# Order of work in a four-layer transformer kernel: a rate for each sequence, and six small shifts

## The chip, the cores and the metric

The kernel runs on one core of a Trainium2 chip. The metric is the device time of one execution in microseconds, from start to end, median of several runs. A core has five engines with a queue of instructions each, worked off in order: TensorE (PE; its weight loads are listed apart as PEld), VectorE (DVE), ScalarE (ACT), GpSimd (POOL), and SyncE (SP), which here only issues transfers. Layers are counted from 1 in the text and from 0 in the code (`l`), sequences likewise (`b`).

## The reference

Four transformer blocks, one after the other, on x of 4 sequences x 512 tokens x 288 channels in float32, with 16 heads of 18, an MLP of 1152, and shift, scale and gate rows computed from a condition vector:

```python
x = _L0_cond_ref(...)   # softmax attention over the tokens; MLP = 4 experts, the 2 best of each token
x = _L1_cond_ref(...)   # softmax attention over the tokens; MLP with gelu
x = _L2_cond_ref(...)   # attention over the heads, token by token (below); MLP with gelu
x = _L3_cond_ref(...)   # softmax attention over the tokens; MLP with gelu

# in _L2_cond_ref: each token's 16 heads attend to one another
attn = jnp.einsum('nthd,ntkd->nthk', q * scale, k)
attn = jax.nn.softmax(attn, axis=-1)
out = jnp.einsum('nthk,ntkd->nthd', attn, v)
out = out.transpose(0, 2, 1, 3).reshape(n, t, d)
x = x + gate_msa[:, None, :] * (out @ proj_w + proj_b)
```

Each block is x + gate * attention(modulate(layernorm(x))) and then x + gate * mlp(modulate(layernorm(x))). In the first block the gate logits choose two experts for each token, and their softmax (the "shares") weighs the two outputs.

## The kernel before, in words

**A planner writes the order.** The program of each engine is laid out in advance by a planner with a counter, `flow["now"]`, that goes up by one at each *gap*. The main line of work (attention steps, expert blocks, MLPs) emits matmuls and calls `gap` or `whole_products` between them; there, side work is put in. Side work stands in lists of generators (`products` for TensorE work; `lanes`, `moves`, `loads`, `spreads`, `casts` for the rest), each with a due time and the keys it reads. `mark(key, delay)` makes a key ready `delay` gaps later; a task starts when its keys are ready. `fill` takes pieces until their costs have used the budget `us` (1.0 for `lanes` and `moves`); a task that is late (due + `SLACK` of 8 gaps passed) goes on until the budget is down to `flow["least"]`. A piece that yields `WAIT` ends that call, so the next piece comes a gap later. Nothing of this costs time on the chip; only the order it leaves counts: what stands ahead of what in each engine's queue.

**Layer 1.** Attention over tokens runs in steps, two gaps each: scores, maxima on VectorE (`maxima`, L721), exponents on ScalarE (L749), value products (L777). A unit is four heads of a sequence and has four steps; its queries and keys come packed by product, and are spread to rows of 32 by transfers (`spread`, L701) issued on SP and POOL. Beside the first steps run the norm of sequence 2, the loads of the projection on POOL (L349 to L355), the clearing of the memory for tokens by expert (L1326, L1332), the product of the gate row (`gate_product`), and the rows for all modulations, half a layer at a time: `load_modulation` (three weight tiles of 288 KB, L405 to L407) and `modulation` (18 matmuls L423, three adds L429, rows written to memory by SP, L479). The next half's loads wait until the half before is `modulated`.

The experts' MLPs follow as 19 blocks of 256 tokens (`expert_block`), each three rounds of "up" (L1710, L1716), gelu on ScalarE (L1722, `hid_b`) and "down" (L1730); a block is 18 gaps. Beside the first blocks the last sequence's tokens are placed, listed (`listing`, VectorE) and scattered, and its shares are computed (`share`: subtract on VectorE L1517, exponent on ScalarE L1519, products on VectorE). `gather` and `combine` bring the outputs back to x, on POOL and VectorE, from block 11 on.

**Layers 2 and 3.** Layer 2's attention is like layer 1's. The MLP of its first sequence is put inside the attention. The MLPs of its sequences 2 to 4, and then all of layer 3's, run as halves of 256 tokens (`half_mlp`: up L1918, L1925, gelu L1929, down L1940; 36 gaps for a sequence; x is updated by ScalarE L1951 and POOL L1952, L1953). Beside them runs layer 3's attention over heads, called the images here: 16 tiles of 128 tokens, each with three products q, k, v (`kept`, L1005), four products and sums on VectorE (`weigh`, L1020, L1026), a softmax (L1030, L1032, exponent on ScalarE L1193), four products with v on POOL (`weighted`, L1039) and their sums on VectorE (`summed`, L1051). After every fourth tile `after(b)` reads the sequence back (L1069), turns and projects it, and norms it for the MLP. The norm of the next sequence (`before(b)`) starts when x of the layer before is marked. These norms compute statistics on VectorE (L512, L513), 1/sqrt on POOL (L520 to L523), and apply them on ScalarE (L537, `xh`), several gaps later (`lag`).

`follow`, called at each gap, keeps the images in step: a credit goes up by `flow["rate"]` at each gap and down by each piece's cost, about VectorE's time for it; pieces that give TensorE work have a negative cost. While it is positive, pieces are emitted.

```python
flow["credit"] = min(flow["credit"] + flow["rate"], 3.0)
...
flow["credit"] -= cost
```

**Layer 4** is again attention over tokens and MLPs. Its first norm and first queries and keys are put beside the end of layer 3's MLPs; its spreads use the tiles that held the images' q, k and v, so they come after the images' end.

The names that the change touches: `RATE`, `flow["rate"]`, `flow["least"]` (in `steps`, `expert_block`), the due time of `norm(l, 0, b)` in `attention`, `share`, the mark of x in `half_mlp`, and the due times of `gate_product` and of the first `modulation` behind the layers' loop.

Of the kernel before, what the change touches and what calls it, by code (L numbers as in the profile page):

```python
# [48 lines left out]
BT = 2 * P  # L49
N_BLOCKS = 2 * B * S // BT + NE - 1  # L50
INSIDE = (44,)
RATE = 1.35
SLACK = 8
EARLY = 5
SHORT = (EARLY + 1, EARLY + 3)
# [5 lines left out]
def tile_dit_blocks(ctx: ExitStack, tc: tile.TileContext, x_in, cond_t, sel_den, sel_b, w_gate, layers, out):  # L61
# [543 lines left out]
    def attention(l, start):  # L605
# [232 lines left out]
        def steps(inside=None, tail=None):  # L838

            end = N_STEPS - LEAD  # L840
            if hidden:
                ready_now = ("set", l, 0)
                while ready.get(ready_now, 1 << 30) > flow["now"]:
                    gap(0.5)
                rebase(start)
            close_all()

            def sum_pair(step, to):
                sum_values(step - 1, to, True, False)
                sum_values(step, to, False, True)  # L850

            flow["least"] = -0.8
            for step in range(first_step, N_STEPS + 1):
                odd = step % 2
                if step == end - 2:
                    flow["least"] = -1e9
                mark(("step", l, step), 0)
                if step < end:
                    flow["others"], flow["turn"] = ((4, 5, 6, 7) if odd and step > 0 else (0, 1, 2, 3)), -1
                if step < 0:  # L860
                    maxima(step, 4 if odd else 0, (4,))
                    flow["others"] = (0, 1, 2, 3) if odd else (4, 5, 6, 7)
                    whole_products(0.4)
                elif step < end:
                    if odd:
                        maxima(step, 4, (1, 1, 2))
                        weights(step, (0, 1, 2, 3), (2, 2))
                        whole_products(1.7)
                    else:
                        weights(step, (0, 1, 2, 3), (1, 1, 2))  # L870
                        maxima(step, 4, (4,))
                        if step:
                            sum_pair(step - 1, other())
                        whole_products(0.3)
                    if inside is not None and step in inside:
                        now = flow["now"]
                        flow["others"] = (7,)
                        inside[step]()
                        close_all()
                        rebase(now)  # L880
                else:
                    if step == end:
                        flow["others"] = (6, 7)
                        if tail is not None:
                            tail()
                    if step < N_STEPS:
                        weights(step, (3, 4, 0, 1), (2, 2))
                    if step == end:
                        sum_pair(step - 1, SUMS)
                    else:  # L890
                        c = (step - 1) % TB
                        sum_values(step - 1, SUMS, c == 0 or step - 1 == end, c == TB - 1)
                    gap(PACE[0])
                    gap(PACE[1])
            close_all()
# [20 lines left out]
        for b in range(B):  # L916
# [1 line left out]
            last = s0 + NG * TB  # L918
            first = hidden and b == 0
            task(  # L920
                lanes, start - 70 if first else at_step(s0 - LEAD - 9 if b else s0 - LEAD - 6),
                [("x", l, 0, b)] + ([("scattered", B - 1)] if l == 1 else []) + ([("step", l, 0)] if b else []),
                norm(l, 0, b, 10 if first and prev == OVER_HEADS else 3),
            )
# [586 lines left out]
    def share(b):  # L1511

        l = lg[:, b * TB : (b + 1) * TB, :]
        both = blocks.pop(("both", b))
        top = tiny([TB, 1], "top")
        nc.vector.tensor_reduce(top, l, AX.X, ALU.max)
        nc.vector.tensor_tensor(l, l, top.to_broadcast([P, TB, NE]), ALU.subtract)  # L1517
        yield 0.4
        nc.scalar.activation(l, l, AF.Exp)  # L1519
        nc.vector.tensor_tensor(l, l, both, ALU.mult)  # L1520
        yield 0.4
        nc.vector.tensor_reduce(top, l, AX.X, ALU.add)
        nc.vector.reciprocal(top, top)
        yield 0.4
        nc.vector.tensor_tensor(l, l, top.to_broadcast([P, TB, NE]), ALU.mult)
        sel = tiny([2, TB, NE], "sel2")
        nc.vector.tensor_tensor(
            sel, chosen[:, :, b * TB : (b + 1) * TB, :], l.unsqueeze(1).to_broadcast([P, 2, TB, NE]), ALU.mult
        )
        yield 0.4  # L1530
        nc.vector.tensor_reduce(shares[:, :, b * TB : (b + 1) * TB], sel, AX.X, ALU.add)
        mark(("shares", b))
        yield 0.4
# [158 lines left out]
    def expert_block(i):  # L1692


        PY, UP = 0, 2
        US = 0.5
        n = tiles_of(i)
        cols = slice(0, n * P)

        def wait_for(key):  # L1700
            while ready.get(key, 1 << 30) > flow["now"]:
                gap(US)

        def up(g, fs):
            wait_for(("third", 3 * i + g))
            rest, b1 = thirds[i][:2]
            w1 = thirds[i, g][0]
            for j in range(3):
                for k in range(KF):
                    nc.tensor.matmul(  # L1710
                        banks[:, UP + j, cols], w1[:, k, j * P : (j + 1) * P], hx[i][:, k, cols], start=k == 0, stop=False
                    )
                gap(US)
            for j in range(3):
                r = slice(j * RC, (j + 1) * RC)
                nc.tensor.matmul(banks[:, UP + j, cols], rest[r, g, :], hx[i][r, KF, cols], start=False, stop=True)  # L1716
            if g == 2:
                mark(("block read", i), 0)
            hid = []
            for j, f in enumerate(fs):  # L1720
                t = work.tile([P, S], F32, tag="ot", bufs=7, name=f"hid_b{i}_{f}")[:, cols]
                nc.scalar.activation(t, banks[:, UP + j, cols], AF.Gelu_apprx_tanh, bias=b1[:, f : f + 1])  # L1722
                hid.append(t)
            return hid

        def down(g, fs, hid):
            w2 = thirds[i, g][1]
            for j, f in enumerate(fs):
                for t in range(n):
                    nc.tensor.matmul(  # L1730
                        banks[:, PY + t, :C], hid[j][:, t * P : (t + 1) * P], w2[:, j, :], start=f == 0, stop=f == NF - 1
                    )
                if f < NF - 1:
                    gap(US)
            mark(("third free", 3 * i + g), 0)
            if g == 2:
                y = blocks["y", i] = work.tile([P, 2, C], F32, tag="upd", bufs=2, name=f"y_b{i}")
                nc.vector.tensor_tensor(
                    y[:, :n], banks[:, PY : PY + n, :C],
                    blocks.pop(("b2", i)).unsqueeze(1).to_broadcast([P, n, C]), ALU.add,  # L1740
                )
                mark(("block out", i))
                gap(US)

        wait_for(("turned", i))
        flow["most"] = -0.05
        for g, fs in enumerate(TRIOS):
            hid = up(g, fs)
            if pending_down:
                pending_down.pop()()  # L1750
            pending_down.append(lambda g=g, fs=fs, hid=hid: down(g, fs, hid))
        flow["most"] = -1e9
# [153 lines left out]
    def half_mlp(l, b, half, hook=None):  # L1906
# [26 lines left out]
        def down(fs, hid):  # L1933
# [14 lines left out]
            if fs[-1] == NF - 1:  # L1948
# [3 lines left out]
                nc.gpsimd.tensor_tensor(y, y, gate[:, b : b + 1, :].to_broadcast([P, 2, C]), ALU.mult)  # L1952
                nc.gpsimd.tensor_tensor(x[:, t0 : t0 + 2, :], x[:, t0 : t0 + 2, :], y, ALU.add)  # L1953
                if half == 1:
                    mark(("x", l + 1, 0, b), 5)
                gap(US)

        for fs in DUOS:
# [47 lines left out]
    for l in range(n_layers):  # L2006
# [7 lines left out]
        if l == 0:  # L2014
            task(products, -100, [("xh", 0, 0, 0)], modulation(l, 0, range(2)))
            task(loads, base, [("spread", l, 2)], load_projection(l))
            task(products, base + 14, [("mod", l, 0), ("ada", 0, 0, 2), ("step", 0, 1)], gate_product(l, 0))
            halves = [(m // 2, m % 2) for m in range(1, 2 * n_layers)]
            for i, half in enumerate(halves):
                free = [("step", 0, 7 * i + 1)] + ([("modulated",) + halves[i - 1]] if i else [])  # L2020
                at = base + 2 * (LEAD + 7 * i) + 2
                task(casts, at, free, load_modulation(*half, range(3), "w2"))
                task(products, at + 10, [("ada",) + half + (2,), ("gate row", 0, 0)], modulation(*half))
        before = [("x", l - 1, 1, B - 1)] if l else []
        task(casts, base + 20, [("gate row", l, 0)] + before + ([("step", 0, 6)] if l == 0 else []), gating(l, 0))
        before = [("x", l, 0, B - 1)] if l else []
# [66 lines left out]
        chain.append([attention_over_heads(OVER_HEADS), False])  # L2093

    lead_attention(1, inside={step: lambda b=b: early_mlp(b) for b, step in enumerate(INSIDE)}, tail=begin_chain)
    flow["rate"] = RATE
    flow["others"] = (4, 7)
    for b in range(len(INSIDE), B):
        while ready.get(("ht", 1, 1, b), 1 << 30) > flow["now"]:
            gap(0.5)  # L2100
        for half in range(2):
# [110 lines left out]
```

## Time and profile before

| | us |
|---|---|
| median of 3 runs | 2200.44 (2199.94 to 2205.9) |
| the profiled execution | 2201.77 |
| its span, first to last instruction | 2200.1 |
| TensorE busy in it | 2050.1 (93%) |
| VectorE busy | 1069.3 (49%) |
| ScalarE busy | 813.9 (37%) |
| POOL busy | 539.9 (25%) |
| granted TensorE clock, mean | 0.973 |

The stages in the span, by the lines that run in them: attention of layer 1 to about 425 us, expert blocks to 847, attention of layer 2 (with one MLP inside) to about 1230, MLPs of layers 2 and 3 with the images to about 1705, attention of layer 4 to about 2050, its MLPs to the end.

In the profile's lists a group reads: line, engine, operation, what it writes and reads; how often; busy time and mean; and the idle time of the engine just before, with what ended it. In a list of waits, "A x L1 <- B y L2: total, times, longest" says that engine A idled before its instruction of line L1 until engine B's of L2 was done. In a table of stretches each engine's busy microseconds and instructions stand in the order PE, weight loads, DVE, ACT, POOL, then the granted clock, the transfers' share and GB/s. In a timeline each row has start, duration, engine, line, and in brackets the idle time before it and what ended it.

### The profile page before, as it was taken

How to read it: one execution, taken by the hardware profiler on the slowest of the kernel's cores; microseconds unless marked ns; L12 is line 12 of the kernel's file. 1: busy time of each engine (PE TensorE's matmuls, PEld its weight loads, DVE VectorE, ACT ScalarE, POOL GpSimd, SP SyncE). 2: the span in 40 equal slices, each digit the busy share in tenths (PEclk: the TensorE clock that was granted, in tenths of full speed). 3: DMA queues.
4: the chain of work that ended last, by engine and by line, in shares of the span. 5: the costliest groups of instructions: out<-in, count | busy, mean ns of one | idle time of the engine just before them, and what ended most of it. 6: DMA issues, size and time to landing. Idle time of an engine off the chain costs nothing.

```text
span 2200.1 us, 28964 instructions
## 1 busy us (share of the span) xinstructions
PE 2050.1 (93%) x10782; PEld 1157.2 (53%) x10782; DVE 1069.3 (49%) x1656; ACT 813.9 (37%) x1333; POOL 539.9 (25%) x584
## 2 busy tenths in 40 slices
PE   7899999899999898999999999889899999999997
PEld 2334434367777474344454677656567444443554
DVE  4556667442002404576445769599630555664101
ACT  2434443422222123545435332333332555455111
POOL 2312131231004013020011295778611101001101
PEclk9989999999999999999999999989999999999999
DMA  3253212355666353000000000312210100000000
GB/s 82 70 171 119 63 57 37 105 167 167 199 200 200 100 167 102 26 24 18 18 6 20 18 9 17 60 26 33 30 48 8 48 20 17 14 18 1 9 14 22
DMA packets 171770, 139.13 MB, mean 63 GB/s; under 512 B 80605, under 2 KB 153749, under 8 KB 171630
## 3 DMA queue, kind: packets, MB, share of 16 engines
q1 hardware_dynamic: 163370, 123.92, 20.1%
q0 software_dynamic: 8064, 13.04, 2.0%
q8 instruction: 86, 1.41, 0.3%
q14 instruction: 54, 0.44, 0.1%
q10 hardware_dynamic: 196, 0.31, 0.0%
HBM read 96.49 MB, written 26.00 MB: 56 GB/s over the span
## 4 chain that ended last, share of the span: by engine, by line
PE 54%; DVE 11%; POOL 5%; issue 3%; ACT 2%; DMA 1%; SPq 0%; POOLq 0%; ACTq 0%; DVEq 0%
PE banks L711 11%; PE banks L640 6%; PE banks L1730 6%; PE banks L1710 5%; PE banks L777 4%; PE banks L1881 4%; PE banks L1858 4%; POOL pv L1039 3%; DVE pq L1020 3%; PE banks L1940 2%; DVE hs L1026 2%; PE banks L828 2%; PE banks L1918 2%; DVE mx L721 2%; DVE ho L1051 1%
## 5 line engine op out<-in xcount | busy, mean ns | idle before, releaser
L721 DVE TENSOR_REDUCE mx<-banks 128x4 f32<-128x2048 f32 (+1 forms) x354 | 423.7, 1238 | 349.7 <-PE banks L711 320.2
L749 ACT ACTIVATE ex<-banks 128x1024 f32<-128x1024 f32 (+1 forms) x471 | 377.6, 865 | 306.3 <-PE banks L711 306.2
L711 PE MATMUL banks<-qk 32*128 32x512 f32 x3072 | 435.0, 625 | 30.1 <-DVE mx L721 12.2
L711 PEld LDWEIGHTS banks<-qk 32*128 32x128 f32 x3072 | 165.9, 184 | 204.5 <-issue 78.2
L1039 POOL TENSOR_TENSOR pv<-hs,qk 128x1152 f32<-128x1152 f32 x60 | 192.4, 3226 | 4.9 <-ACT hs L1193 4.9
L777 PE MATMUL banks<-ex,va 128*32 128x512 f32 x1536 | 191.2, 611 | 2.5 <-ACT ex L749 2.5
L1730 PE MATMUL banks<-w_b,hid_b 128*128 128x288 f32 x648 | 178.9, 418 | 0.0
L640 PE MATMUL banks<-ht,wqk 96*128 96x512 f32 (+1 forms) x348 | 166.4, 611 | 9.1 <-DVE mx L721 8.7
L1710 PE MATMUL banks<-block,w_b 128*128 128x256 f32 (+1 forms) x684 | 158.2, 378 | 4.1 <-ACT hid_b L1722 4.1
L1918 PE MATMUL banks<-ht,w 128*128 128x256 f32 x504 | 131.4, 397 | 25.3 <-ACT hid L1929 25.2
L1722 ACT ACTIVATE hid_b<-banks,b_b 128x256 f32<-128x256 f32 (+1 forms) x171 | 66.9, 461 | 233.5 <-PE banks L1716 145.4
L1940 PE MATMUL banks<-w,hid 128*128 128x288 f32 x504 | 145.1, 423 | 0.0
L1730 PEld LDWEIGHTS banks<-w_b,hid_b 128*128 128x128 f32 x648 | 116.7, 190 | 50.4 <-issue 23.3
L1710 PEld LDWEIGHTS banks<-block,w_b 128*128 128x128 f32 x684 | 126.2, 195 | 29.6 <-issue 6.8
L763 POOL DMA_DIRECT2D qk<-maxima x48 | 29.7, 620 | 378.8 <-ACT maxima L762 362.4
L1918 PEld LDWEIGHTS banks<-ht,w 128*128 128x128 f32 x504 | 97.7, 199 | 46.9 <-ACT hid L1929 28.2
L599 POOL TENSOR_TENSOR x<-x,upd_a 128x288 f32<-128x288 f32 x48 | 38.6, 805 | 314.4 <-DVE upd_a L598 292.3
L640 PEld LDWEIGHTS banks<-ht,wqk 96*128 96x128 f32 (+1 forms) x348 | 60.9, 186 | 100.0 <-issue 55.8
L1940 PEld LDWEIGHTS banks<-w,hid 128*128 128x128 f32 x504 | 90.0, 190 | 44.2 <-issue 25.5
L777 PEld LDWEIGHTS banks<-ex,va 128*32 128x32 f32 x1536 | 40.1, 110 | 136.6 <-issue 69.1
L1929 ACT ACTIVATE hid<-banks,b 128x256 f32<-128x256 f32 x126 | 53.6, 471 | 133.0 <-PE banks L1925 127.7
L1051 DVE TENSOR_REDUCE ho<-pv 128x72 f32<-128x1152 f32 x64 | 85.2, 1337 | 31.4 <-POOL pv L1039 31.3
(244 smaller groups left out, 2461.9 us busy)
## 6 DMA issues: line engine op xcount, KB each, us to landing
w_b<-in_w SPq DMA_DIRECT2D x57, 432.0 KB
w_b<-in_w SPq DMA_DIRECT2D x57, 384.0 KB
qk<-qc SPq DMA_DIRECT2D x270, 38.0 KB
wa<-in_wada SPq DMA_DIRECT2D x24, 288.0 KB
x_mem<-zeros SPq DMA_DIRECT2D x21, 256.0 KB
y_mem<-zeros SPq DMA_DIRECT2D x21, 256.0 KB
block<-x_mem SPq DMA_DIRECT2D x17, 288.0 KB
y_mem<-y_b SPq DMA_DIRECT2D x17, 288.0 KB
```

Source lines behind the costliest of these rows:

```text
L640: nc.tensor.matmul(to, st(rows, k), mv(rows, k), start=k == 0, stop=k == NK - 1)
L711: nc.tensor.matmul(to, qk[u][r, of, c * P : (c + 1) * P], qk[u][r, 1 - of, :], start=True, stop=True)
L721: nc.vector.tensor_reduce(mxs[u % 2][:, j : j + n, c], banks[:, bank + j : bank + j + n, :], AX.X, ALU.max)
L749: nc.scalar.activation(ex[step, j // 2][:, j % 2 : j % 2 + n, :], banks[:, to[j] : to[j] + n, :], AF.Exp, scale=SCALE)
L777: nc.tensor.matmul(to[j * HP : (j + 1) * HP, :], vas[0][:, c, at : at + HP], ex[step, j // 2][:, j % 2, :], start=first, stop=last,)
L1039: engine.tensor_tensor(prod, sc[i][:, hs, :].unsqueeze(2).to_broadcast([P, GH, HD, NH]), qkv[i, 2].rearrange("p h d -> p d h").unsqueeze(1 ...
L1051: nc.vector.tensor_reduce(o[i][:, hs, :], pv.pop((i, g)), AX.X, ALU.add)
L1710: nc.tensor.matmul(banks[:, UP + j, cols], w1[:, k, j * P : (j + 1) * P], hx[i][:, k, cols], start=k == 0, stop=False)
L1730: nc.tensor.matmul(banks[:, PY + t, :C], hid[j][:, t * P : (t + 1) * P], w2[:, j, :], start=f == 0, stop=f == NF - 1)
L1858: nc.tensor.matmul(banks[:, 4 + j, :], full[:, k, (f % 3) * P : (f % 3 + 1) * P], h[:, k, :], start=k == 0, stop=False,)
L1918: nc.tensor.matmul(banks[:, UP + j, :BT], full[:, k, (f % 3) * P : (f % 3 + 1) * P], h[:, k, s], start=k == 0, stop=False,)
L1940: nc.tensor.matmul(banks[:, PY + t, :C], hf[:, t * P : (t + 1) * P], w["w2"][f // 3][:, f % 3, :], start=False, stop=f == NF - 1,)
```

## The change

Seven edits, all to the order. The rate of the images is 0.9, 1.2 and 1.6 beside the MLPs of layer 2's sequences 2, 3 and 4, where it was 1.35, and stays at 1.6 beside layer 3's. Late pieces stop at a budget of -0.3 in the attention of layers 2 to 4 and in the expert blocks from the ninth on, where they stopped at -0.8 and not at all. Layer 1's norm of sequence 2 is due three steps earlier. The last sequence's share waits three gaps between subtract and exponent. x is marked 8 gaps, not 5, after a sequence's second half. The gate product of layer 1 is due at base + 21 instead of base + 14, its second half's modulation 18 gaps after its loads instead of 10.

```diff
-RATE = 1.35
+RATES = (1.0, 0.9, 1.2, 1.6)
...
-            flow["least"] = -0.8
+            flow["least"] = -0.3 if l else -0.8
...
             task(
-                lanes, start - 70 if first else at_step(s0 - LEAD - 9 if b else s0 - LEAD - 6),
+                lanes, start - 70 if first else at_step(s0 - LEAD - (9 if l or b > 1 else 12) if b else s0 - LEAD - 6),
                 [("x", l, 0, b)] + ([("scattered", B - 1)] if l == 1 else []) + ([("step", l, 0)] if b else []),
                 norm(l, 0, b, 10 if first and prev == OVER_HEADS else 3),
             )
...
         nc.vector.tensor_tensor(l, l, top.to_broadcast([P, TB, NE]), ALU.subtract)
         yield 0.4
+        for _ in range(3 if b == B - 1 else 0):
+            yield WAIT
         nc.scalar.activation(l, l, AF.Exp)
...
         wait_for(("turned", i))
         flow["most"] = -0.05
+        if i > EARLY + 2:
+            flow["least"] = -0.3
         for g, fs in enumerate(TRIOS):
...
                 if half == 1:
-                    mark(("x", l + 1, 0, b), 5)
+                    mark(("x", l + 1, 0, b), 8)
...
-            task(products, base + 14, [("mod", l, 0), ("ada", 0, 0, 2), ("step", 0, 1)], gate_product(l, 0))
+            task(products, base + 2 * (LEAD + 4) + 1, [("mod", l, 0), ("ada", 0, 0, 2), ("step", 0, 1)], gate_product(l, 0))
...
-                task(products, at + 10, [("ada",) + half + (2,), ("gate row", 0, 0)], modulation(*half))
+                task(products, at + (10 if i else 18), [("ada",) + half + (2,), ("gate row", 0, 0)], modulation(*half))
...
-    flow["rate"] = RATE
     flow["others"] = (4, 7)
     for b in range(len(INSIDE), B):
+        flow["rate"] = RATES[b]
```

## The prediction

> **What bounds the kernel now.** I read the share of busy time first, then the idle times of TensorE one by one, then for each what ended it, and last the five engines in stretches of the images' stage.
>
> ```profile
> PE   7899999899999898999999999889899999999997
> ...
> PE 54%; DVE 11%; POOL 5%; issue 3%; ACT 2%; DMA 1%; SPq 0%; POOLq 0%; ACTq 0%; DVEq 0%
> ```
>
> TensorE is busy almost everywhere, so a change can win only what TensorE idles, and what it then loses to a slower clock. The list of its idle times holds some 30 over 0.8 us, about 101 us together. The ones this change can reach are three: 4.9 us at 104.8 in the first attention, 3.5 us at 502.9 in the expert blocks, and those of the stage in which layer 3's attention over heads ("the images") runs beside the MLPs of layers 2 and 3, 1226 to 1600: 10.0, 2.3, 8.3, 4.8 and 9.7 us. In that stage the waits read:
>
> ```profile
> PE banks L1918 <- ACT hid L1929: 25.2, 6, 10.0
> ...
> ACT xh L537 <- POOL off L523: 20.3, 4, 8.3
> ...
> ACT qc L666 <- DMA qk<-qc: 15.4, 1, 15.4
> ```
>
> (engine, line, for whom; total us, times, longest.) TensorE waits for a gelu (L1929) that itself waits for nothing: it stands in ScalarE's queue behind a norm's xh (L537), which waits for POOL, which waits for statistics on a VectorE that is behind. The stretches show when VectorE is behind:
>
> ```profile
> 1245.00:1319.00 74.00, 72.65 (x328) 52.63 (x327) 53.93 (x59) 27.61 (x52) 63.75 (x34) 1.00 0.06 7
> 1319.00:1379.00 60.00, 59.85 (x265) 44.02 (x264) 58.31 (x63) 16.05 (x33) 35.41 (x22) 1.00 0.09 16
> 1379.00:1413.00 34.00, 24.18 (x112) 18.41 (x112) 11.83 (x12) 16.71 (x30) 31.22 (x22) 0.85 0.28 39
> 1413.00:1550.00 137.00, 120.35 (x510) 88.14 (x511) 134.49 (x138) 49.91 (x91) 104.18 (x60) 0.91 0.23 40
> 1600.00:1700.00 100.00, 100.00 (x453) 68.39 (x453) 17.31 (x33) 25.22 (x54) 18.17 (x21) 0.99 0.10 29
> ```
>
> (length; PE, weight loads, DVE, ACT, POOL; clock.) VectorE is full from 1319 to 1379 and again from 1413 to 1550 (134.5 of 137 us), and has 20 us to spare before 1319. After 1600 TensorE is at 100% and nothing of the images is left.
>
> **The change, part by part.**
>
> *Share of the last sequence (L1519 behind three WAITs).* Now:
>
> ```profile
> 494.80 1.28 ACT L1519 ACT_TABLE_LOAD   x1
> ...
> 504.40 0.22 ACT L1519 ACTIVATE lg<-lg 128x16 f32<-128x16 f32 x1 [8.32 <-DVE lg L1517]
> 504.63 1.28 ACT L1722 ACT_TABLE_LOAD   x1
> ...
> 506.45 5.49 PE L1710 MATMUL banks<-block,w_b 128*128 128x256 f32 x12 [3.52 <-ACT hid_b L1722]
> ```
>
> The exponent blocks ScalarE 8.3 us while VectorE works off the listing; the gelu behind it is late. By the code it moves from planner gap 390 to 393, that is past the gelus of block 2's last trio. The wait is gone: 3.52, plus the slow clock after it (this group took 5.49 where the same took 2.75 at 496.4, its rest 1.02 instead of 0.71): 6.6 us. VectorE's subtract stays at 504.2, so the next gelu is ready at 504.6 + 1.28 = 505.9, and TensorE asks for it at about 502.9 + 2.75 + 0.71 = 506.4: a margin of 0.5 us only. I take -5.0; ends 0 to -6.6, and +1.3 if VectorE, waiting for the exponent at L1520, holds up the block copy behind it.
>
> *First attention (norm of sequence 2 three steps earlier; gate product and second modulation later).* The score at 104.8 waits for the spread of unit 4. That was issued at 104 because SP stood 21.8 us at L1332 behind a POOL memset, POOL stood 19.4 us at a norm's rstd, and its projection loads came in between (waits of the DMA queue, then of the engines, 90 to 125):
>
> ```profile
> SPq L1332 <- POOL zeros L1326: 21.8, 1, 21.8
> ```
>
> ```profile
> POOL rstd L528 <- DVE rstd L527: 19.4, 1, 19.4
> ```
>
> Sixteen score matmuls take 2.0 us elsewhere and 14.0 here (103.63 to 117.67): 12.0 us lost, 2.8 more at the slow clock until 123.4 (3.64 for 1.92, 1.12 for 0.60, 2.54 for 2.00). What changes: the norm's nine pieces go out in three fills instead of five, its transposes one step earlier, one of two qk products (2.7 us) with them; the modulation (18 matmuls in 1.73 us, 3 DVE adds of 1.41, one of 0.30, three SP transfers) moves from step 5 to step 9, and with it the nine loads behind it on SP (wa, bada; issued at 107.3 to 119) from just behind the spread to after step 10. But the spread itself is ready at the same planner gap (229), still behind POOL's loads. So it comes 1.7 us earlier, without the wa loads beside it: between the first head's landing (109.67) and the next (113.84) lie 4.2 us, of which I give 3.3 to them. Together -5.0; ends -14.8 (all of it) and +2.5 (four pieces, 2.5 us, between two maxima that TensorE waits for at 63). The gate product (6 matmuls, 1.71 us, one add, one transfer) only moves from step 1 to 4; the projection it gates comes at step 19. The Trainium skill ("TensorE: Matmul & The Clock Gate", Part 1: The HAM clock gate) says the clock halves after an idle window of about 3.4 us; here it was 0.50 from 270.2 to 273.6 after a wait of only 2.65 us. By the page a stall cut below 3.4 us would cost itself alone, and this term would be some 2 us better; by the row it still costs a slow stretch, and the sum goes by the row.
>
> *Late VectorE pieces (least -0.3).* Pieces of 0.6 stop after three instead of four (attention) or after all six (blocks from 8 on). The combine at gap 613 has all six before the copy of gap 615 as before, so the 5.2 us wait at 766 stays; the one at 577 lets the copy pass two pairs (1.8 us), where TensorE waited for nothing; the one at 685 stays in one step. 0; ends -2 and +1.
>
> *Images.* A sequence's MLP has 36 gaps; two f-tiles are four gaps and 4.50 us (L1918 at 1366.07, next at 1370.57), so a gap is 1.125 us of TensorE. The images get 36 x (0.9 + 1.2 + 1.6) = 133 instead of 146 us of credit in layer 2's MLPs, and 1.6 after. They are gated thrice: tiles 4, 8 and 12 wait for a norm of x behind MLP 1, 2 and 3, each now 3 gaps later. Slower at first costs nothing: before, by the planner's counts, tile 3 was shifted at gap 842 and tile 4 came only at 871. But tiles 2 and 3 are then still being summed when tile 4 starts (4 of 8 pieces), so their first sequence ends near gap 880, not 868, and its second norm no longer falls on top of the third sequence's first norm. Those two together are the 10 us stall:
>
> ```profile
> 1382.33 2.18 ACT L537 ACTIVATE xh<-x,off,rstd 128x288 f32<-128x288 f32 x4 [8.32 <-POOL off L523]
> ...
> 1388.82 2.08 PE L1918 MATMUL banks<-ht,w 128*128 128x256 f32 x4 [9.97 <-ACT hid L1929]
> ```
>
> It is worth 9.97 + 2.2 (half of 1388.8 to 1393.2 at clock 0.5) = 12.2; I take -9, since at 1.6 POOL falls behind (a product of 3.23 us per 3.2 of credit is 2.0 gaps, 2.25 us). End 0.
>
> Against it: in layer 3's MLPs 61 gaps x 1.35 = 82 of credit become 82 / 1.6 = 51.5 gaps. VectorE was full there at 1.35 already, so the same work has 9.5 gaps less TensorE work beside it: +10.7; and the gate for sequence 4 and the MLP behind it comes 3 gaps later: +3.4. Ends 0 (if freed time lets VectorE start earlier) and +14.1.
>
> The last stall, 9.66 us at 1587.8 plus 2.0 at the slow clock, is layer 4's queries: their spread stands on SP behind the images' last read (L1065 waits 11.2 for VectorE, L1069 5.7 for the write). With the images done ten gaps sooner and layer 4's first norm 3 gaps later (mark 8) that read is over first. ScalarE's own four issues took 8.6 us there, so not all goes: -6; ends 0 and -11.7.
>
> *Sum:* -5.0 - 5.0 + 0 - 9 + 10.7 + 3.4 - 6 = -10.9. From the profiled execution's 2201.8 us (span 2200.1 and 1.7 around it) that is **2191 us**; the median of the runs shown is 2200.4, so 0.4% under it.
>
> **The rivals.**
>
> *1.6 binds (slower).* Place: layer 3's MLPs of sequences 1 and 2. Price +14.1, and the stalls of 12.2 and 11.7 stay, as VectorE is again behind whenever a norm is due; with the share's -5 that is +9.1: **2211**. It decides once VectorE is behind by more than a norm's lag of three gaps (3.4 us) at the end of layer 2's MLPs. For it: 134.5 of 137 us. Against: VectorE idled 22 of the 34 us from 1379 to 1413, behind the very stall that I expect to go.
>
> *The gates decide, not the rates.* Tiles 4, 8 and 12 start by the norms whatever the rate; nothing moves in the images, and the first attention keeps its queue order: only the share acts, **2197**. For it: the spread at gap 229 as before. Against: 1.6 against 1.35 changes 60 gaps in a row.
>
> *The stalls go and the rate hides.* Share -6.6, first attention -12, -12.2, -11.7, only +3.4 paid: -39, **2163**. For it: after 1600 there are 100 us of plain MLP that could take the shift. Against: TensorE's work is fixed, what leaves the images' stage must be free of stalls there.
>
> **How the numbers follow.** About 0.3% (6.6 us) is what a measurement tells from no change: faster is below 2193.8, slower above 2207.0. Forecast 0.45 (0.39 of it faster, 0.06 within), 1.6 binds 0.27 (0.02 within), gates decide 0.12 (0.03 faster), stalls go 0.16: faster 0.58, within 0.17, slower 0.25. The forecast's own range is 2181 to 2199; the range for 8 in 10 reaches to the two outer cases: 2163 to 2215.
>
> **What would show it.** Share: no idle of TensorE over 1 us at 500 to 510, ScalarE not waiting for L1517. First attention: TensorE's wait for the spread near 105 below 3 us, wa loads after it. Images: no xh wait of 8 us near 1380; VectorE full until its end; fewer MLP matmuls beside it; no ScalarE wait on qk<-qc of 15 us. It is wrong if VectorE's full stretch is broken by new waits for POOL, if the stall at 1380 only moves, or if stalls appear at places I priced at nothing: the blocks after 8, and the norms of the last layer.

## The result, and the profile after

The changed kernel takes **2216.9 us** (median of 5 runs, 2210.6 to 2220.6), the kernel before 2200.4 in runs beside it: ratio 1.0071, 95% interval 1.0054 to 1.0088. It became slower where 2191 was forecast, and the time lies just outside the range. The profiled execution after took 2215.47 us, its span 2213.6.

The share of busy time by slices and the chain of waits, after:

```profile
span 2213.6 us, 28966 instructions
...
PE   7899999899999998999999999886899999999997
...
PE 66%; DVE 13%; issue 3%; ACT 2%; POOL 2%; DMA 1%; SPq 0%; POOLq 0%; ACTq 0%; DVEq 0%
```

In the row of PE the 28th of the 40 slices (1494 to 1549 us) reads 6, where it read 9. The chain has more of VectorE (13%, was 11%). The waits from 1226 to 1600 (engine, line, for whom; total us, times, longest), after. The lines of the MLP halves are now 4 higher, so L1922 is the "up" that was L1918, and L1933 its gelu:

```profile
PE banks L1922 <- ACT hid L1933: 36.0, 8, 13.4
...
ACT xh L537 <- POOL off L523: 27.7, 5, 9.5
...
ACT hs L1193 <- DVE hs L1032: 13.3, 1, 13.3
```

TensorE's wait for a gelu has grown from 25.2 us to 36.0, the norms' xh from 20.3 to 27.7, and ScalarE's wait for VectorE's subtract in the softmax of the images' last tile from 4.4 to 13.3. The same stretches as before (length; PE, weight loads, DVE, ACT, POOL; clock, transfers):

```profile
1319.00:1379.00 60.00, 57.48 (x249) 41.82 (x249) 58.93 (x57) 17.34 (x37) 35.46 (x23) 0.97 0.08 16
1379.00:1413.00 34.00, 33.77 (x153) 25.13 (x152) 21.73 (x23) 12.73 (x24) 29.29 (x13) 1.00 0.40 67
1413.00:1550.00 137.00, 105.26 (x444) 76.10 (x442) 130.54 (x132) 50.22 (x88) 114.38 (x69) 0.88 0.20 33
```

Two things are to be seen. From 1379 to 1413 TensorE is now busy 33.8 of 34 us at full clock, where it was 24.2: the stall of 10 us at 1380 went, as forecast. From 1413 to 1550 it is busy 105 us of 137 instead of 120, at 0.88 instead of 0.91, while VectorE is nearly as full as before (130.5 us, was 134.5).

**Where the time went.** I set marks by the k-th instance of the same instruction in both traces. The stage with the images is taken from the first gelu of the MLP of layer 2's second sequence to the last gelu of layer 3's MLPs:

| us | before | after | difference |
|---|---|---|---|
| 60th maxima (layer 1's attention) | 214.3 | 210.1 | -4.2 |
| 119th maxima | 389.6 | 389.5 | -0.1 |
| first gelu of the stage | 1231.5 | 1224.0 | -7.5 |
| images' last sum (L1051) | 1576.2 | 1570.4 | -5.8 |
| last gelu of the stage | 1711.0 | 1724.9 | +13.9 |
| **length of the stage** | **479.5** | **500.9** | **+21.4** |
| TensorE idle in it | 38.6 | 50.2 | +11.6 |
| TensorE busy at half clock in it | 23.5 | 34.5 | +11.0 |

So in these two executions 7.5 us are won ahead of the stage and 21.4 lost in it; nothing happens behind it. The 7.5 prove little by themselves: two kernels below that change nothing ahead of the stage (layer 2's rates alone, all three rates alone) reached its first gelu at 1228.9 and at 1243.4. The images themselves take as long as before (344.7 us from the first gelu to their last sum before, 346.4 after). What changed is how much of TensorE's work got done beside them. Of the 21.4 us, 11.6 are idle time of TensorE; the 11.0 us more at half clock are worth about half of that, 5.5 us (an estimate). The rest is not accounted for. The largest new stall stands in the timeline of after (start, duration, engine, line; in brackets the idle time before it and what ended it):

```profile
1528.48 1.35 DVE L1026 TENSOR_REDUCE hs<-pq 128x64 f32<-128x1152 f32 x1
1529.75 1.34 DVE L1051 TENSOR_REDUCE ho<-pv 128x72 f32<-128x1152 f32 x1
...
1531.22 6.25 POOL L1039 TENSOR_TENSOR pv<-hs,qk 128x1152 f32<-128x1152 f32 x2
1531.45 6.31 DVE L1032 TENSOR_TENSOR hs<-hs,ht 128x256 f32<-128x256 f32 x1
...
1537.80 0.42 ACT L1193 ACTIVATE hs<-hs 128x256 f32<-128x256 f32 x1 [13.28 <-DVE hs L1032]
...
1539.52 0.84 ACT L1933 ACTIVATE hid<-banks,b 128x256 f32<-128x256 f32 x2
...
1540.05 2.50 PE L1922 MATMUL banks<-ht,w 128*128 128x256 f32 x5 [13.42 <-ACT hid L1933]
```

ScalarE has had nothing to do since it loaded the exponent's table at 1523.2 (1.28 us), because an exponent stands ahead of the gelus in its queue; VectorE has five instructions of about 1.35 us and a maximum of 0.41 to do before it comes to the subtract at 1531.45 (6.9 us behind), and the subtract then takes 6.31 us instead of 0.53. TensorE waits 13.42 us. By the profile the clock is at half from 1529.8 to 1543.4, mostly within that wait, so that the first 3.4 us of TensorE's work behind it run slow as well.

### The profile page after: what moved, and what is told of

Its sections match the earlier page's. It is cut to its first block, busy times and chain, and to the rows that moved or that the text cites. A ratio compares the mean times of both kernels' runs of the same rounds, so it can differ in the third digit from the quotient of the medians.

```text
span 2213.6 us, 28966 instructions
## 1 busy us (share of the span) xinstructions
PE 2061.4 (93%) x10782; PEld 1157.0 (52%) x10782; DVE 1067.5 (48%) x1656; ACT 814.2 (37%) x1333; POOL 539.6 (24%) x584
## 4 chain that ended last, share of the span: by engine, by line
PE 66%; DVE 13%; issue 3%; ACT 2%; POOL 2%; DMA 1%; SPq 0%; POOLq 0%; ACTq 0%; DVEq 0%
PE banks L711 13%; PE banks L640 8%; PE banks L1732 7%; PE banks L1712 6%; PE banks L777 5%; PE banks L1944 4%; PE banks L1885 4%; PE banks L1862 4%; PE banks L1922 3%; DVE mx L721 3%; PE banks L828 3%; DVE pq L1020 2%; DVE ho L1051 2%; PE banks L1005 2%; PE banks L1718 1%
## 5 line engine op out<-in xcount | busy, mean ns | idle before, releaser
L711 PE MATMUL banks<-qk 32*128 32x512 f32 x3072 | 444.1, 632 | 28.1 <-DVE mx L721 12.3
L640 PE MATMUL banks<-ht,wqk 96*128 96x512 f32 (+1 forms) x348 | 166.3, 610 | 10.1 <-DVE mx L721 9.7
L1922 PE MATMUL banks<-ht,w 128*128 128x256 f32 x504 | 132.3, 398 | 39.2 <-ACT hid L1933 39.2
L1922 PEld LDWEIGHTS banks<-ht,w 128*128 128x128 f32 x504 | 97.3, 198 | 63.9 <-ACT hid L1933 43.7
L763 POOL DMA_DIRECT2D qk<-maxima x48 | 29.8, 621 | 409.9 <-ACT maxima L762 409.8
L599 POOL TENSOR_TENSOR x<-x,upd_a 128x288 f32<-128x288 f32 x48 | 38.6, 806 | 316.8 <-DVE upd_a L598 289.1
L640 PEld LDWEIGHTS banks<-ht,wqk 96*128 96x128 f32 (+1 forms) x348 | 60.6, 185 | 101.2 <-issue 55.6
L1933 ACT ACTIVATE hid<-banks,b 128x256 f32<-128x256 f32 x126 | 53.6, 471 | 149.8 <-PE banks L1929 136.0
L1020 DVE TENSOR_TENSOR pq<-banks,qk 128x1152 f32<-128x1152 f32 x64 | 86.2, 1347 | 19.8 <-PE banks L1005 19.4
```

Source lines behind the costliest of these rows:

```text
L640: nc.tensor.matmul(to, st(rows, k), mv(rows, k), start=k == 0, stop=k == NK - 1)
L711: nc.tensor.matmul(to, qk[u][r, of, c * P : (c + 1) * P], qk[u][r, 1 - of, :], start=True, stop=True)
L1020: nc.vector.tensor_tensor(prod, QUERIES[i % 2][:, :C].rearrange("p (h d) -> p h d", d=HD)[:, hs, :].unsqueeze(2).to_broadcast([P, GH, NH, ...
L1922: nc.tensor.matmul(banks[:, UP + j, :BT], full[:, k, (f % 3) * P : (f % 3 + 1) * P], h[:, k, s], start=k == 0, stop=False,)
```

## The experiments

Ratios are to runs of the kernel before on the same chip, with 95% intervals. The groups ran on different chips, on which the kernel before took 2201.8 to 2209.5 us, so for what lies in the images' stage I also give the **stage's length** from the profile, which is steadier: the changed kernel profiled twice gave 500.9 and 500.7. Two kernels that differ only outside the stage agreed within 0.2 us in one case (486.2 and 486.1) and within 3.5 in others (479.5 to 482.9 in five kernels whose order of instructions in the stage is the same); differences under 3.5 us are not read. Each length is of one execution.

**1. The rates undone, or alone.** All seven edits but 1.35 throughout; and the kernel before with the rates alone:

```diff
-RATES = (1.0, 0.9, 1.2, 1.6)
+RATES = (1.0, 1.35, 1.35, 1.35)
```

> The changed kernel with the rate at 1.35 beside all MLPs again, the other six edits kept. Theory 'the rate binds' (a higher rate beside layer 3's MLPs only takes MLP work from beside a VectorE that is full): the 7.5 us gained before the images' MLPs stay and the stage's loss goes: 2193 us, ratio to before 0.995 to 0.998. Rival 'the mark of 8 gaps or the late-piece limits cost the time': stays near 2215, ratio above 1.004.

> The kernel before with only the rates 0.9, 1.2, 1.6. Theory 'the rate binds': the stage's loss of some 21 us without the 7.5 us gained ahead of it: 2215 to 2224 us, ratio 1.007 to 1.011. Rival 'the mark or the limits cost the time': 2195 to 2203, ratio within 0.003 of 1.

Undone: 0.9955 (0.9937 to 0.9973), stage 477.7. Alone: 1.0027 (1.0017 to 1.0037), stage 486.2. The first says that without the new rates the change wins; the second missed the first theory's expectation by a wide margin and lies at the edge of the rival's: the rates alone cost 6.7 us in the stage, not 21. Neither theory was right alone; something costs only together with the rates.

**2. Which of the rates.** The new ones beside layer 2's MLPs with 1.35 beside layer 3's, and the reverse:

```diff
     flush(1)
+    flow["rate"] = 1.35
     for b in range(B):
```

> The changed kernel with 0.9, 1.2 and 1.6 beside layer 2's MLPs but 1.35 beside layer 3's. If 1.6 beside layer 3's MLPs is what costs: about 10 gaps of MLP come back beside the images, 2195 to 2203 us. If the slow start beside layer 2's MLPs (0.9, 1.2: images' work moved later) is what costs: stays at 2212 or above.

> The changed kernel with 1.35 beside layer 2's MLPs and 1.6 beside layer 3's: the other half of the rates. If 1.6 beside layer 3's MLPs is what costs: slower than the version with 1.35 throughout by some 10 us, 2203 or above. If the slow start is what costs: 2193 to 2197, like the version with 1.35 throughout.

Layer 2's rates alone of the two: 0.9948 (0.9935 to 0.9961), stage 475.5; at 2189.9 us it is faster than either theory expected. Layer 3's 1.6 alone: 1.0047 (1.0033 to 1.006), stage 500.7, the whole loss of the changed kernel in the stage. The cost sits at 1.6 beside layer 3's MLPs, here with the mark at 8; the slow start beside layer 2's costs nothing.

**3. Slower still beside layer 3.**

```diff
+    flow["rate"] = 1.2   # the second kernel: 1.1
```

> The changed kernel with 1.2 beside layer 3's MLPs. A gap is 1.125 us of TensorE, so at 1.6 the program runs ahead of VectorE by 0.475 us per gap, at 1.35 by 0.225, at 1.2 by 0.075. Theory 'the rate beyond 1.125 comes back as stalls': idle time of TensorE in the stage falls below the 32 us of the version with 1.35, 2180 to 2188 us. Rival 'the images' end then comes too late for layer 4's first norm, queries and spreads': 2192 us or above, with a wait longer than the 6.3 us at 1579.

> The changed kernel with 1.1 beside layer 3's MLPs, just under the gap of 1.125 us. Theory 'the rate beyond 1.125 comes back as stalls': no slower than at 1.2, 2178 to 2188. Rival 'the images' end comes too late': slower than at 1.2, 2192 or above, VectorE with gaps between 1440 and 1550.

0.9974 (0.9958 to 0.999) with a stage of 485.2, and 0.9958 (0.9943 to 0.9972) with 488.7. The first theory's expectations missed (2202.0 and 2199.1 us): it does not go on below 1.35. At 1.1 the images end 354.4 us after the stage's first gelu, where they took 343.3 at 1.2 and 342.4 at 1.35, and from 1440 to 1550 VectorE is busy 100.2 us of 110, at 1.35 105.1: there the rival's reason holds. At 1.2 the images end as early as at 1.35, yet TensorE idles 35.1 us in the stage instead of 28.8 (6.0 and 6.6 us ahead of L1922 at 1511 and 1561, 3.8 at layer 4's first scores). At 1.1 it idles 33.0 us, but 51.5 us of its work run at half clock, where it was 29.5 at 1.35. By the stage 1.35 is the best of 1.1, 1.2, 1.35 and 1.6, and the order of stalls is not monotone in the rate; the intervals of the ratios of 1.1, 1.2 and 1.35 overlap and do not rank them.

**4. The subtract beside POOL's products.** Left out of the computation on the last tile alone:

```diff
-            engine = nc.vector if i == len(tiles) - 1 else nc.gpsimd
-            engine.tensor_tensor(sc[i], sc[i], top.to_broadcast([P, NH, NH]), ALU.subtract)
+            if i == len(tiles) - 1:
+                return
+            nc.gpsimd.tensor_tensor(sc[i], sc[i], top.to_broadcast([P, NH, NH]), ALU.subtract)
```

> The changed kernel without the subtraction of the maximum on the images' last tile alone (left out of the computation; the softmax of that tile is then taken of the scores as they are). In the changed kernel this VectorE subtract took 6.31 us beside two POOL products, and TensorE idled 13.42 us behind it. Theory 'the subtract held up by POOL sets the size of that stall': TensorE's idle there falls to about 7 us and the slow clock behind it with it, 6 to 10 us in all: 2207 to 2211 us. Rival 'VectorE is behind anyway, the stall only moves': 2214 us or above, with as much idle time of TensorE between 1500 and 1600.

In its timeline (lines one higher) the exponent now waits for the maximum itself:

```profile
1528.57 0.41 DVE L1030 TENSOR_REDUCE ht<-hs 128x16 f32<-128x256 f32 x1
...
1529.01 0.42 ACT L1194 ACTIVATE hs<-hs 128x256 f32<-128x256 f32 x1 [6.95 <-DVE ht L1030]
...
1531.26 3.35 PE L1923 MATMUL banks<-ht,w 128*128 128x256 f32 x7 [5.47 <-ACT hid L1934]
```

ScalarE's wait falls from 13.28 to 6.95 us and TensorE's from 13.42 to 5.47, so the held-up subtract made 6.3 us of the first, and a VectorE that is behind the other 7. (In the second profile of the changed kernel the subtract again took 6.31 us, and TensorE waited 11.85.) The stage became only 3.5 us shorter (497.2), at the limit of what is read; the ratio was 1.0023 (1.0007 to 1.004), on another chip than the changed kernel's runs. Both theories hold a part: the stall shrinks as expected and TensorE idles 40.6 us in the stage instead of 50.2, but 46.9 us of its work run at half clock instead of 34.5, which takes most of the gain back.

**5. The mark.** At 5 again, everywhere; at 8 for only one of the two layers; and the changed kernel itself on the chip of these:

```diff
-                    mark(("x", l + 1, 0, b), 8)
+                    mark(("x", l + 1, 0, b), 5)   # others: 8 if l == 1 else 5, and 5 if l == 1 else 8
```

> The changed kernel with x marked 5 gaps after a sequence's second half again. The rates alone made 1.0027 of the kernel before, the whole change 1.0071, though the other edits win 10 us at 1.35. Theory 'the later mark costs where the rate is 1.6 (the norm and the MLP behind it come three gaps later)': 2202 to 2211. Rival 'the mark does nothing': 2213 to 2219.

> The changed kernel itself, on the chip of the runs beside it, so that they can be compared without a change of chip: ratio to before 1.005 to 1.009.

> The changed kernel with the later mark (8) only for layer 2's x, which gates the images' tiles 4, 8 and 12; layer 3's x, which gates layer 4's first norm, marked after 5 gaps again. If the later gate of the images is what costs beside the rate of 1.6: near the changed kernel, at most 4 us under it, with TensorE's idle times of 3 to 6 us at 1421 to 1438 still there. If the later norm of layer 4 is what costs: some 12 us under the changed kernel, and no idle time of 7 us at 1572.

> The changed kernel with the later mark only for layer 3's x (layer 4's first norm), layer 2's x marked after 5 gaps again. If the later gate of the images is what costs: 10 us or more under the changed kernel, within 4 us of the version with the mark at 5 throughout. If the later norm of layer 4 is what costs: within 4 us of the changed kernel.

| 1.6 beside layer 3, mark of x | ratio | stage, us |
|---|---|---|
| 8 for both layers (the change) | 1.0071 (1.0048 to 1.0095) | 500.7 |
| 8 for layer 2's x only | 1.0002 (0.9982 to 1.0022) | 492.2 |
| 8 for layer 3's x only | 1.0029 (1.0011 to 1.0046) | 495.9 |
| 5 for both | 0.9956 (0.9938 to 0.9974) | 486.1 |

The runs with 5 for both are those of another chip than the three above them, and at 2199.8 us they lie below both of their expectations. By the stage the mark costs 14.6 us beside the rate of 1.6. Where the other layer's mark is at 8 already, layer 3's x costs 8.5 us and layer 2's 4.8; where it is at 5, 9.8 and 6.1: the two nearly add up. By the ratios of the one chip they would be some 15 and 9 us, each give or take 7. The expectations had put the cost on one of them. How layer 3's mark does it is seen in two timelines. With 8:

```profile
1579.15 2.18 ACT L537 ACTIVATE xh<-x,off,rstd 128x288 f32<-128x288 f32 x4 [9.59 <-POOL off L523]
1582.19 3.78 PE L1922 MATMUL banks<-ht,w 128*128 128x256 f32 x8 [7.54 <-ACT hid L1933]
...
1592.51 2.17 ACT L537 ACTIVATE xh<-x,off,rstd 128x288 f32<-128x288 f32 x4
...
1609.72 1.47 PE L581 MATMUL banks<-ident,xh 128*96 128x128 f32 x12
1612.82 2.74 PE L640 MATMUL banks<-ht,wqk 96*128 96x512 f32 x6
```

With 5 for layer 3's x:

```profile
1572.28 2.17 ACT L537 ACTIVATE xh<-x,off,rstd 128x288 f32<-128x288 f32 x4
...
1579.03 1.47 PE L581 MATMUL banks<-ident,xh 128*96 128x128 f32 x12
1582.63 2.74 PE L640 MATMUL banks<-ht,wqk 96*128 96x512 f32 x6
1582.71 2.18 ACT L537 ACTIVATE xh<-x,off,rstd 128x288 f32<-128x288 f32 x4 [0.93 <-POOL off L523]
```

The norm of layer 4 is the one whose 12 transposes (L581) stand right ahead of the first queries (L640); the other is the norm ahead of layer 3's MLP of sequence 3. With 5, layer 4's comes first, its xh waits for nothing, and its queries give TensorE work at 1582.6. With 8 the two norms change places: the norm of layer 3 goes first and waits 9.59 us for statistics that come behind the images' last sums, the gelus wait in ScalarE's queue behind it, TensorE idles 7.54 us, and the queries come 30 us later (1612.8).

**6. Both taken back.** 1.35 beside layer 3 and the mark at 5, with the other edits; and without layer 2's rates too:

> The changed kernel with 1.35 beside layer 3's MLPs and the mark at 5: the rate of 1.6 and the later mark both taken back. If the mark costs only beside a rate of 1.6: like the version with 1.35 and mark 8, ratio to before 0.993 to 0.997. If the two costs add: 10 us under that version, ratio 0.988 to 0.991.

> The changed kernel with 1.35 throughout and the mark at 5: share, first attention and limits alone. If these three make the gain and the rates of layer 2 little: ratio 0.993 to 0.997, the stage with the images as long as before (479 us from the first gelu of its MLPs to the last). If the rates 0.9, 1.2 and 1.6 beside layer 2's MLPs are needed for the gain of the version with 1.35 beside layer 3's and mark 5 (0.9913, stage 473): 5 us or more slower than that one.

0.9913 (0.9884 to 0.9941), stage 473.2; and 0.996 (0.9941 to 0.9979), stage 480.1. The first has the lowest ratio of all, 2187.7 us where the kernel before took 2205.6 beside it, though the intervals of others overlap with its own; the ratio lies between its two expectations. Its stage is 2.3 us shorter than with the mark at 8, within what is not read: beside 1.35 the later mark costs little or nothing. The trace of the version with 1.35 and the mark at 8 shows why: there the norms keep their places, layer 4's xh starting at 1554.7 and waiting for nothing, the other's at 1567.8. Without the rates in layer 2 the stage is as long as before.

**7. The other parts, each alone, on the kernel before.**

> The kernel before with only the three waits in the last sequence's share. Predicted step: TensorE's wait of 3.52 us at 503 and the slow clock behind it go: -5.0 us, ratio 0.996 to 0.999. Rival 'the wait only moves on': ratio 0.999 to 1.001, with an idle time of 2 us or more within 20 us behind it.

> The kernel before with only the earlier norm of sequence 2, the later gate product and the later second modulation of layer 1. Predicted step: -5.0 us. The profile of the changed kernel shows 4.1 us gained by 214 us and none left by 390. Theory 'gained, then given back by slow-clock stretches behind the next waits': maxima at 210 some 3 us earlier than before, at 390 level, ratio 0.998 to 1.001. Rival 'that was chance of one execution': gain stays, ratio 0.996 to 0.998.

> The kernel before with only the limits of -0.3 on late pieces (attention of layers 2 to 4, expert blocks from the ninth). Predicted step: 0, ratio 0.999 to 1.001. Rival 'the limits shorten the waits near 754 and 766 in the expert blocks' (the changed kernel had 1.2 us less there, and one of 2.06 us at 724 less): -3 to -6 us, ratio 0.997 to 0.9985.

Share: 0.997 (0.9956 to 0.9983), that is 6.6 us. First attention: 0.9999 (0.9984 to 1.0015). Limits: 0.9995 (0.9979 to 1.001). For the first attention TensorE's wait for the spread falls from 4.90 to 2.34 us and the half clock behind it from 13.7 to 10.2, the 60th maxima comes 2.7 us earlier than before, the 119th 1.7 later. The shorter wait is steady: 4.5 to 5.1 us in the six profiles without this part, at most 2.5 in the fourteen with it. Where its gain goes is not shown: in the six without it, the 60th maxima came between 211.1 and 216.2 us and the 119th between 386.3 and 395.8, so one execution against one can't tell a gain given back from chance.

**8. Layer 2's rates alone, and with the share.**

```diff
+RATES = (1.0, 0.9, 1.2, 1.6)
...
+        flow["rate"] = RATES[b]
...
+    flow["rate"] = 1.35   # beside layer 3's MLPs
```

> The kernel before with only 0.9, 1.2 and 1.6 beside layer 2's MLPs and 1.35 beside layer 3's as before; no other edit. If layer 2's rates alone carry the gain of the stage: the stage 473 us long (479.5 before), ratio 0.995 to 0.998. If the other edits are needed for it: stage 477 us or longer, ratio 0.998 or above.

> The kernel before with layer 2's rates (0.9, 1.2, 1.6, then 1.35) and the share's three waits alone. If these two parts are all that helps: ratio 0.990 to 0.994, as with all seven edits, the mark at 5 and 1.35 beside layer 3. If first attention or limits add: 0.995 or above.

0.995 (0.9932 to 0.9969), stage 471.5; and 0.9942 (0.9922 to 0.9962), stage 473.5. Layer 2's rates alone take 8.0 us out of the stage. The second lies between its two expectations, and its interval overlaps that of the version with all the other edits; the 6.6 us of the share can't be told on top of the rates. In the stage waits of the rates alone (1226 to 1600):

```profile
ACT qc L666 <- DMA qk<-qc: 15.8, 1, 15.8
...
PE banks L1918 <- ACT hid L1929: 12.7, 7, 5.3
...
PE banks L581 <- ACT qc L666: 10.1, 1, 10.1
```

The wait for gelus is halved (25.2 to 12.7), and the last stall, for layer 4's queries, stays at 10.1 us (9.66 before).

## Why the prediction was wrong

By its own steps, with what the runs showed for each, in microseconds; the parts of the stage in stage length:

| step of the prediction | forecast | measured |
|---|---|---|
| share | -5.0 | -6.6 (alone) |
| first attention | -5.0 | 0, between -3.5 and +3.3 (alone) |
| late pieces | 0 | -1, between -4.6 and +2.2 (alone) |
| the stall at 1380 | -9 | -8.0 (layer 2's rates alone, stage 479.5 to 471.5) |
| fewer gaps beside a full VectorE | +10.7 | +14.8 (1.6 beside layer 3 added, 471.5 to 486.2; what it does to the last stall is in it) |
| the gate 3 gaps later | +3.4 | +4.8 to +6.1 (mark of layer 2's x) |
| last stall, by images sooner and mark 8 | -6 | the stall itself 9.7 to 2.7; the mark of layer 3's x +8.5 to +9.8; both marks together +14.6 |
| sum | -10.9 | +13.8 |

The measured sum agrees with the ratio: 0.71% of 2200.4 is 15.6 us (11.9 to 19.4).

The last row takes the rate at +14.8 and both marks at +14.6. For these two the prediction had +8.1 in all (10.7 + 3.4 - 6); they measured +29.4, and that is 21 of the 25 us of error.

**The step that failed** is the one on the last stall: "With the images done ten gaps sooner and layer 4's first norm 3 gaps later (mark 8) that read is over first", priced at -6 with ends 0 and -11.7. What it says of its own stall came true, though not by images that end sooner in time: with the mark at 5 their last sum comes 339.9 and 340.0 us after the first gelu beside 1.6, 335.2 to 338.6 beside 1.35. ScalarE's wait behind layer 4's spreads, 15.4 us before, in the changed kernel (1226 to 1640):

```profile
ACT qc L666 <- DMA qk<-qc: 7.6, 1, 7.6
```

TensorE's wait behind it was 9.66 us before and 10.1 with layer 2's rates alone; it is 5.0 with 1.6 added (ahead of L1918, at 1603) and 2.71 in the changed kernel (ahead of L1922, at 1626). What the step left out is the price of the later mark. It counted the mark as harmless, even helpful, because it makes layer 4's norm later, and did not ask which norm comes in its place. The new stall of 7.4 us at 1572 (7.54 in the second profile), behind the norm that now goes first, is that price, and the mark of layer 3's x costs 8.5 to 9.8 us where the end at 0 was the worst that was allowed. Stalls at "the norms of the last layer" stood among the prediction's signs of being wrong.

The term of the gaps had the right mechanism but too small a size: +14.8 with the last stall's fall in it, where 10.7 and a part of the -6 were put. In the stage TensorE idles 38.4 us with 1.6 added, 29.8 without, and 32.8 us of its work run at half clock, where it was 22.6; the term had counted neither a new stall nor the clock. The gaps taken from beside the images appear as a stall of 12.7 us (13.4 in the changed kernel), and it is a wait of ScalarE for VectorE: the lag in VectorE's work that the rival "1.6 binds" named. That rival had the place right. Its bound that the stalls of 12.2 and 11.7 would stay was wrong: the first went by layer 2's rates, and the second shrank. Its time, 2211, was nearest, in part by luck, as these stalls stand in for the price of the marks, of which it had only 3.4. It was put at 0.27 because VectorE's idle time from 1379 to 1413 spoke against it; VectorE is now busy 21.7 of these 34 us instead of 11.8, and that did not keep the new stall out of layer 3's MLPs.

The first attention's term was read correctly as far as the spread (TensorE's wait under 3 us, a shorter slow stretch), but the 5 us did not reach the end. In the trace of after two waits that are the same as before, 2.65 us at 263 and 3.12 at 343, are followed by 6.8 us at half clock each, instead of 3.4. In the rule of the Trainium skill that stood there ("TensorE: Matmul & The Clock Gate", Part 1: The HAM clock gate), a window of about 3.4 us is also said to run free; that the same wait of 2.65 us was followed by 3.4 us at half clock before, by 6.8 after and by 10.2 in the second profile of the changed kernel agrees with that. That the clock took the gain back is not shown.

The stall at 1380 went by the mechanism forecast: the norm's xh that waited 8.32 us there waits for nothing in the changed kernel. The share was right in place and nearly in size: no wait of TensorE is left at 503, as in the timeline of after, where the exponent now stands behind the trio's gelus:

```profile
498.54 1.21 ACT L1724 ACTIVATE hid_b<-banks,b_b 128x256 f32<-128x256 f32 x3 [5.13 <-PE banks L1718]
499.77 1.28 ACT L1521 ACT_TABLE_LOAD   x1
...
501.40 2.75 PE L1712 MATMUL banks<-block,w_b 128*128 128x256 f32 x12
...
503.03 0.22 ACT L1521 ACTIVATE lg<-lg 128x16 f32<-128x16 f32 x1 [1.98 <-DVE lg L1517]
```

The margin of 0.5 us that I feared did not bind. The late pieces, put at 0, measured within their interval of it.

What stays open: why 1.2 beside layer 3's MLPs is worse than 1.35 although the images end as early; how the mark of layer 2's x makes its cost, which no timeline here follows; and what becomes of the first attention's gain.

## What to carry to other kernels

When an engine was full here, putting its work into the program at a higher rate did not speed it up; it made the in-order queues that share it wait longer, so ask how far the program runs ahead of the full engine, and what stands behind its consumer. When a piece is made later, ask what then stands in its old place in each queue: here the two norms changed places, and that cost more than the delay itself. Where the total scatters by several microseconds between executions, compare the length of the one stage that the edit touches, between the same two instructions, and take more than one execution of it where a few microseconds decide.

## What the runs showed of the hardware

A VectorE subtract of two operands in the on-chip memory (128x256) stands once in each kernel but that of section 4 (L1032). It took 0.42 to 0.56 us in nine profiles, where it began in the last 0.3 us of a POOL instruction, and 1.53 and 1.66 in two, where it began beside a POOL sum into x (1.40 us) and ended just after it. In seven it began 0.1 to 0.3 us after a POOL product had begun: it took 6.27 to 6.32 us beside two products that followed each other without a break (6.25 us together in the changed kernel), and 9.39 beside three in the kernel with 1.6 in layer 3 only. In these seven it did not get its turn between one POOL product and the next. In the kernel with 1.1 it did: it began 2.2 us into a product, took 1.18 us and ended 0.3 us after that product, and the next product took 3.36 us, the one before 3.14. What tells these cases apart is not shown. VectorE's products L1020, with one operand in the banks that the matmuls write, took 1.35 us beside the same POOL products, and its reductions 1.34.

The Trainium skill ("SBUF — State Buffer", Who interferes with whom) says that a VectorE instruction with two SBUF inputs contends with a GpSimd instruction that reads SBUF, and (SBUF: two separate sides) that whichever starts first holds the shared ports for the whole instruction. The rows above agree, and in seven profiles go further: there the hold lasted over two and three instructions in a row.
